# Cross-attention on one core: values of two quads in one run, rows of x by halves in one room, output-projection steps dealt anew

## The chip, the cores and the metric

The kernel runs on one core of one Trainium2 chip. The metric is the device time of one launch in microseconds (us), the median of several runs. All data are 32-bit floats.

The engines go by the names of the profile: PE is TensorE (matrix products), PEld its weight loads, DVE is VectorE, ACT is ScalarE, POOL is GpSimd, and SP is SyncE, whose queue issues nearly all DMA transfers. Each engine runs its own instructions in the order in which the program gives them, and waits by semaphores for what other engines hand it.

## The reference

Eight batches of 256 rows with 1024 features; 32 heads of 32 features each. `ctx` serves as keys and as values.

```python
xn = (x - mean(x)) * rsqrt(var(x) + 1e-5) * gamma + beta
Q  = split_heads(xn @ Wq.T)                     # 8 x 32 heads x 256 x 32
K = V = split_heads(ctx)
scores = einsum('bhsd,bhtd->bhst', Q, K) / sqrt(32), masked over t
attn   = einsum('bhst,bhtd->bhsd', softmax(scores), V)
out    = x + merge_heads(attn) @ Wout.T         # 8 x 256 x 1024
```

## The kernel before

**Quads and slots.** Four heads (128 features) are a *quad*; a batch has eight, all batches 64. The main loop (`for n in range(N)`, N = 64) does one *slot* per quad. The code writes i for the slot's place in its batch of output work: b, i = divmod(n - 8, 8). The order of instructions on every engine is written out by hand (the pool's scheduler is off). In slot n TensorE does, in this order:

1. `scores(n + 1)` (L493): scores of the next quad, 8 matmuls into the four banks of `ps_s`;
2. `project_steps(n, 0)`;
3. `values(n - 2)` (L643): softmax times V of the quad two slots back, 64 matmul records in the trace, into the two banks of `ps_v`;
4. `project_steps(n, 1)`;
5. in slots i = 2 to 7 and 0 `query_product` (L216, tile `pq`): one of the seven products that make Q for a later batch;
6. behind the softmax of quad n + 1 in the program, `project_steps(n, 2)`.

**Projections.** Both projections are done by a scheme with seven products of half-size blocks (A11, A12, S2, S3, A22, S1, S4, in this order for the output), with sums of blocks formed on GpSimd (`sum_at`, `sum_x`). The output projection of a batch is 28 *steps* (seven products of four chunks; a step is one call of `product`, L216, tile `po`), dealt over the nine slots that follow the batch's attention. `STEPS[i]` says how many steps stand at places 0, 1 and 2 of slot i:

```python
STEPS = ((0, 0, 0), (0, 7, 0), (0, 1, 2), (0, 2, 2), (0, 2, 1), (0, 1, 2), (0, 0, 3), (0, 1, 2),
         (0, 2, 0))
```

All products of the output share one bank (`ps_o`) and, for the first, the bank of `ps_q`. Between products the sum is evacuated: `keep_p1` (ScalarE, L735, slot i = 1), `take` and `store` (VectorE, L765 and L769, slots 2, 3, 4, 6, 7, 8; store(1,0) in i = 6, store(1,1) in i = 7). The batch before the last (b = 6) has its own deal, `ENDS`, its own evacuation by `copy_po` (ScalarE, L745, slots 59 to 63), and the last batch's steps (`po_last`, `po_end`) stand in slots 59 to 62 and after the loop.

**Softmax.** `softmax(n + 1)` runs in slot n. VectorE: eight reductions that add the mask and find the row's extreme (L531), reciprocals (L542), four block transposes `blocks` into pT (L556), the evacuations above, the query copies `copy_product` (L475, L470), the mask (`mask_bias`, L483, at the end of slots i = 6). ScalarE: exponentials (L535), `copy_at` (L656), which takes the finished values of a quad out of `ps_v` right behind the first exponentials, and `aside` (L562), a copy of half of pT into `pc`. GpSimd: the normalization (L550). The tail of a softmax (last transpose, last copy aside, and on SP's queue the moves between pT and pc, L621 and L625, with the loads of k, L135, and v, L143) stands at its end; for quads after 56 it is held back into the next softmax.

**Rows of x.** Every batch's x passes through: load (L129), statistics (`ln_stats`, L234 to L239, on VectorE, 1.6 us for a half of 128 rows), normalization (`ln_norm`, L255, ScalarE), block transposes into `xe` (`blocks_x`, L323, VectorE), and sixteen moves into xnT on SP's queue (`move_x`, L339, in slots first - 6 to first - 4). `first` = 8(b - 1) + 2 is the slot of the batch's first query product. The tables `loads`, `stats`, `norms`, `trans`, `moves` and `at_end` give the slot of each, per half s = 0, 1. x and xe take turns in two rooms of a pool `xp` of 8 KB per partition each.

Of the kernel before, what the change touches and what calls it, by code (L numbers as in the profile page):

```python
# [46 lines left out]
F32 = mybir.dt.float32  # L47
# [12 lines left out]
def xattn_kernel(  # L60
# [25 lines left out]
    N = B * NQ  # L86

    const = ctx.enter_context(tc.tile_pool(name="const", bufs=1))
    xp = ctx.enter_context(tc.tile_pool(name="xp", bufs=2))
    rp = ctx.enter_context(tc.tile_pool(name="rp", bufs=4))  # L90
    lnp = ctx.enter_context(tc.tile_pool(name="lnp", bufs=2))
    kp = ctx.enter_context(tc.tile_pool(name="kp", bufs=2))
# [1 line left out]
    atp = ctx.enter_context(tc.tile_pool(name="atp", bufs=3))  # L94
    ep = ctx.enter_context(tc.tile_pool(name="ep", bufs=4))
    ptp = ctx.enter_context(tc.tile_pool(name="ptp", bufs=3))
    asp = ctx.enter_context(tc.tile_pool(name="asp", bufs=3))
    up = ctx.enter_context(tc.tile_pool(name="up", bufs=1))
    sm = ctx.enter_context(tc.tile_pool(name="sm", bufs=8))
    dram = ctx.enter_context(tc.tile_pool(name="dram", bufs=1, space=bass.MemoryType.DRAM))  # L100
# [18 lines left out]
        nc.tensor.transpose(busy, ident, ident)  # L119


    xs, ks, vs, rs = {}, {}, {}, {}

    def load_x(b, s, h=None, queue=nc.sync):

        if b not in xs:
            xs[b] = xp.tile([P, NS, D], F32, tag="x", name=f"x_{b}")
        cols = ds(0, D) if h is None else ts(h, 512)
        queue.dma_start(xs[b][:, s, cols], x[b, ts(s, P), cols])  # L129

    def load_k(n):

# [91 lines left out]
    def ln_stats(b, s, parts=range(3), later=None):  # L224


        if s == 0 and 0 in parts:
            mvs[b] = sm.tile([P, NS, 2], F32, tag="mv", name=f"mv_{b}", bufs=2)
            rstds[b] = sm.tile([P, NS], F32, tag="rstd", name=f"rstd_{b}", bufs=2)
        if 0 in parts:  # L230
            sts[b, s] = sm.tile([P, 2, 6], F32, tag="st", name=f"st_{b}_{s}", bufs=2)
        for h in range(2):
            if h in parts:
                nc.vector.bn_stats(sts[b, s][:, h, :], xs[b][:, s, ts(h, 512)])  # L234
        if 2 not in parts:
            return
        nc.vector.bn_aggr(mvs[b][:, s, :], sts[b, s].rearrange("p h k -> p (h k)"))
        ve = sm.tile([P, 1], F32, tag="ve", name=f"ve_{b}_{s}", bufs=2)
        nc.vector.tensor_scalar(ve, mvs[b][:, s, 1:2], LN_EPS, None, ALU.add)  # L239

        def pow_():
            nc.gpsimd.tensor_tensor(rstds[b][:, s : s + 1], ve, mhalf[:, :1], ALU.pow)

        if later is None:
            pow_()
        else:
            later.append(pow_)

    def ln_norm(b, s, engine):
        if engine is nc.scalar:  # L250
            shift = sm.tile([P, 1], F32, tag="shift", name=f"shift_{b}_{s}", bufs=2)
            nc.gpsimd.tensor_scalar(
                shift, mvs[b][:, s, 0:1], rstds[b][:, s : s + 1], -1.0, ALU.mult, ALU.mult
            )
            engine.activation(  # L255
                xs[b][:, s, :], xs[b][:, s, :], AF.Identity,
                bias=shift, scale=rstds[b][:, s : s + 1],
            )
            return
        engine.tensor_scalar(  # L260
            xs[b][:, s, :], xs[b][:, s, :], mvs[b][:, s, 0:1], rstds[b][:, s : s + 1],
            ALU.subtract, ALU.mult,
        )

# [4 lines left out]
    def transpose_x0(s, diag=None):  # L269

        pool, tag, k = (ps_v, "pv", NC // 2) if diag is None else (ps_s, "sc", 2)
        for g in range(NC // k):
            pt = pool.tile([P, k, P], F32, tag=tag, name=f"px0_{s}_{g}")
            for i in range(k):
                px0[s, k * g + i] = pt[:, i, :]
                chunk = xs[0][:, s, ts(k * g + i, P)]
                if diag is None:
                    nc.tensor.transpose(pt[:, i, :], chunk, ident)
                else:
                    nc.tensor.matmul(pt[:, i, :], chunk, diag, start=True, stop=True)  # L280
# [24 lines left out]
    def transpose_x1(p):  # L305

        if p == 0:
            tile_ = lnp.tile([P, NC * (S + 1)], F32, tag="xnT", name="xnT_1")
            px1["to"] = tile_[:, : NC * S].rearrange("p (c t) -> p c t", c=NC)
            xnTs[1] = lambda c: px1["to"][:, c, :]  # L310
        pt = px1[p] = ps_v.tile([P, 2, S], F32, tag="pv", name=f"px1_{p}")
        for i in range(2):
            for s in range(NS):
                nc.tensor.transpose(pt[:, i, ts(s, P)], xs[1][:, s, ts(2 * p + i, P)], ident)  # L314

    def copy_x1(p):
        nc.scalar.copy(px1["to"][:, ts(p, 2), :], px1.pop(p))
# [1 line left out]
    def blocks_x(b, s):  # L319

        if s == 0:
            xes[b] = xp.tile([P, NA, NC, NS, K], F32, tag="x", name=f"xe_{b}")
        nc.vector.transpose(  # L323
            xes[b][:, :, :, s, :],
            xs[b][:, s, :].rearrange("p (c q k) -> p q c k", c=NC, q=NA),
        )

    def move_x(b, part):
# [178 lines left out]
    def softmax_parts(n, copies=(), ahead=(), between=(), hooks={}, fill=()):  # L507
# [9 lines left out]
                fill.pop(0)()  # L517

        pss = scs[n]
        pT = pTs[n] = ptp.tile([P, 2, NI, NH, NS, K], F32, tag="pT", name=f"pT_{n}")  # L520
        pc = asp.tile([P, NI, NH, NS, K], F32, tag="pc", name=f"pc_{n}")
        es, mns, dens = {}, {}, {}

        def exps(j, part=range(NS)):
# [107 lines left out]
            tail()  # L632
        yield

    def values(n):
        pvs[n] = [
            ps_v.tile([P, 2, NS, K], F32, tag="pv", name=f"pv_{n}_{r}") for r in range(2)
        ]
        pT = pTs.pop(n)
        for i in range(NI):  # L640
            for j in range(NH):
                for r in range(2):
                    nc.tensor.matmul(  # L643
                        pvs[n][r][j * HD : (j + 1) * HD],
                        vs[n - n % 2][ts(r, 2 * K), i, ds(n % 2 * P + j * HD, HD)],
                        pT[ts(r, 2 * K), :, i, j, :, :],
                        start=(i == 0), stop=(i == NI - 1),
                    )

    def copy_at(n):  # L650
        b, c = divmod(n, NQ)
# [3 lines left out]
        for r, pv in enumerate(pvs.pop(n)):  # L655
# [19 lines left out]
    P1_ASIDE = (0, 1, 2, 3, 4, 5)  # L675
    STEPS = ((0, 0, 0), (0, 7, 0), (0, 1, 2), (0, 2, 2), (0, 2, 1), (0, 1, 2), (0, 0, 3), (0, 1, 2),
             (0, 2, 0))
    ENDS = ((0, 0, 2), (0, 0, 5), (0, 0, 5)) + ((0, 0, 4),) * 4 + ((0, 0, 0),)
    ENDS_TO = {2: (0, 0), 3: (0, 1), 4: (1, 1), 5: (1, 0), 6: (1, 1), 7: (0, 1)}

    def steps_of(b):
        if b == B - 2:
            return ENDS
        return STEPS

    assert all(sum(map(sum, steps_of(b))) == len(PRODUCTS) * NK for b in range(B - 1))

# [200 lines left out]


    ln_stats(0, 0)  # L890
    x0 = xs[0][:, 0, :]
    mean = mvs[0][:, 0, 0:1]
    nc.vector.tensor_scalar(x0, x0, mean, None, ALU.subtract)
    diag = ring[:, 0, 1, :]
# [53 lines left out]
    for n in range(N):  # L948
# [19 lines left out]
        if n in (2, 4):  # L968
            between.append(partial(load_wo, B21, n // 2 - 1))
        if n == N - 4:  # L970
            again = xp.tile([P, NS, D], F32, tag="x", name="x_again")
            for s in range(NS):
                between.append(partial(nc.sync.dma_start, again[:, s, :], x[B - 1, ts(s, P), :]))

# [8 lines left out]
                place = 0 if i in (3, 4, 6) or i < 3 and what is not add_p1 else "soon" if i == 2 else 1  # L983
                hooks.setdefault(place, []).append(partial(what, one, *args))
        if n >= 2:
            values(n - 2)
        project_steps(n, 1)
        copies = [partial(copy_q, q) for q in new_q]
        if n in halves and n % 2 == 0:
# [26 lines left out]
                make_q(q)  # L1016
                copy_q(q)
        else:
            copy_at(n - 2)
# [160 lines left out]
```

## Time and profile before

| | |
|---|---|
| runs | 563.6, 563.45, 562.49 us; median 563.45 |
| profiled execution | 562.29 us, its span 560.5 us |
| granted TensorE clock | 1.00 |
| busy: PE, DVE, ACT, POOL | 555.1, 466.3, 423.7, 392.9 us |
| DMA moved | 119.30 MB, mean 213 GB/s |

A row of a timeline gives the start in us from the start of the span, the duration, engine, source line, operation, output<-inputs by the program's names, shapes, and how many instructions (x16) were taken together; in square brackets stands the idle time ahead and what ended it. The 32-bit matmuls show as several records each: sixteen records are one `scores`, four are one step of the output projection. Matmuls are pipelined, so a row's duration runs over into the next row's; what a run occupies is read from start to start.

### The profile page before, as it was taken

How to read it: one execution, taken by the hardware profiler on the slowest of the kernel's cores; microseconds unless marked ns; L12 is line 12 of the kernel's file. 1: busy time of each engine (PE TensorE's matmuls, PEld its weight loads, DVE VectorE, ACT ScalarE, POOL GpSimd, SP SyncE). 2: the span in 40 equal slices, each digit the busy share in tenths (PEclk: the TensorE clock that was granted, in tenths of full speed). 3: DMA queues.
4: the chain of work that ended last, by engine and by line, in shares of the span. 5: the costliest groups of instructions: out<-in, count | busy, mean ns of one | idle time of the engine just before them, and what ended most of it. 6: DMA issues, size and time to landing. Idle time of an engine off the chain costs nothing.

```text
span 560.5 us, 24339 instructions
## 1 busy us (share of the span) xinstructions
PE 555.1 (99%) x9334; PEld 357.0 (64%) x9334; DVE 466.3 (83%) x1716; ACT 423.7 (76%) x1464; POOL 392.9 (70%) x635
## 2 busy tenths in 40 slices
PE   8999999999999999999999999999999999999997
PEld 7666665767656767567765676566766766744443
DVE  5979889999998888988898888988888878879823
ACT  3699999998769867797777877778776876869920
POOL 1688887999797666867568666777648657448780
PEclk9999999999999999999999999999999999999999
DMA  8967657957678767877778767788667874536752
GB/s 305 397 188 209 184 150 235 319 179 223 207 253 246 246 183 223 259 204 232 217 232 233 207 186 233 221 233 239 176 166 249 244 228 130 149 91 182 209 169 76
DMA packets 47236, 119.30 MB, mean 213 GB/s; under 512 B 8976, under 2 KB 9744, under 8 KB 47120
## 3 DMA queue, kind: packets, MB, share of 16 engines
q1 hardware_dynamic: 46832, 117.48, 69.5%
q8 instruction: 74, 1.21, 1.0%
q14 instruction: 42, 0.34, 0.2%
q10 hardware_dynamic: 288, 0.27, 0.1%
HBM read 66.33 MB, written 11.53 MB: 139 GB/s over the span
## 4 chain that ended last, share of the span: by engine, by line
PE 98%; DVE 1%; DMA 1%; ACT 0%; POOL 0%; issue 0%; POOLq 0%
PE po_S L216 20%; PE pq_A L216 19%; PE pv L643 12%; PE sc L493 12%; PE po_A L216 11%; PE pq L216 10%; PE pq_S L216 7%; PE po_end L216 3%; PE po_last L216 1%; DMA x<-in_x_dram 1%; PE po_end_s L216 0%; PE px L280 0%; PE px L314 0%; ACT e L535 0%; DVE st L234 0%; DVE xnT L289 0%
## 5 line engine op out<-in xcount | busy, mean ns | idle before, releaser
L550 POOL TENSOR_SCALAR e<-e,rden 128x256 f32<-128x256 f32 x466 | 215.5, 479 | 124.2 <-DVE rden L542 121.7
L535 ACT ACTIVATE e<-e,mn 128x256 f32<-128x256 f32 x512 | 254.0, 501 | 43.6 <-DVE mn L531 43.1
L556 DVE STREAM_TRANSPOSE pT<-e 128x512 f32<-128x512 f32 x256 | 178.9, 703 | 36.6 <-POOL e L550 27.5
L531 DVE CUSTOM_DVE_ANT_0 e<-sc,mb 128x256 f32<-128x256 f32 x512 | 185.3, 416 | 23.8 <-PE sc L493 23.3
L562 ACT COPY pc<-pT 128x512 f32<-128x512 f32 x128 | 78.9, 616 | 52.2 <-DVE pT L556 34.5
L535 ACT ACTIVATION_READ_ACCUMULATOR e<-e,mn 128x1 f32 x512 | 98.2, 192 | 0.0
L493 PEld LDWEIGHTS sc<-k,qa 32*128 32x128 f32 x1024 | 46.1, 184 | 45.6 <-issue 22.4
L643 PE MATMUL pv<-pT,v 64*32 64x128 f32 x4096 | 74.2, 274 | 0.0
L493 PE MATMUL sc<-k,qa 32*128 32x256 f32 x1024 | 73.6, 400 | 0.2 <-ACT qa L301 0.2
L216 PE MATMUL po_S<-wo,at 128*64 128x512 f32 x304 | 73.5, 598 | 0.0
L643 PEld LDWEIGHTS pv<-pT,v 64*32 64x32 f32 x4096 | 57.1, 105 | 22.7 <-issue 9.6
L216 PE MATMUL po_A<-wo,at 128*64 128x512 f32 x256 | 58.6, 598 | 0.0
L216 PE MATMUL pq<-xnT,wq 128*64 128x256 f32 (+3 forms) x544 | 58.4, 369 | 0.0
L216 PEld LDWEIGHTS pq_A<-xnT,wq 128*64 128x64 f32 x832 | 46.3, 137 | 7.4 <-issue 6.3
L216 PE MATMUL po_S<-wo,s 128*64 128x512 f32 x208 | 49.5, 598 | 0.0
L216 PEld LDWEIGHTS pq<-xnT,wq 128*64 128x64 f32 x544 | 36.8, 136 | 18.9 <-issue 1.8
L216 PE MATMUL pq_A<-xnT,wq 128*64 128x128 f32 x832 | 47.6, 273 | 0.0
L542 DVE RECIPROCAL rden<-den 128x2 f32<-128x2 f32 x256 | 38.3, 150 | 5.8 <-ACT e L535 4.9
L531 DVE DVE_READ_ACCUMULATOR2_ANT mn<- 128x1 f32 x512 | 42.6, 83 | 0.0
L216 PEld LDWEIGHTS po_A<-wo,at 128*64 128x64 f32 x256 | 16.9, 136 | 30.0 <-issue 29.1
L216 PEld LDWEIGHTS po_S<-wo,at 128*64 128x64 f32 x304 | 19.3, 136 | 22.6 <-issue 22.6
L656 ACT COPY at<-pv 128x128 f32<-128x128 f32 x128 | 26.2, 254 | 8.7 <-PE pv L643 8.7
(99 smaller groups left out, 645.4 us busy)
## 6 DMA issues: line engine op xcount, KB each, us to landing
v<-in_kv_dram SPq DMA_DIRECT2D x32, 512.0 KB, 4.8
pT<-pT SPq DMA_DIRECT2D x128, 128.0 KB, 3.3
pT<-pc SPq DMA_DIRECT2D x128, 128.0 KB, 4.1
ring<-kept_T SPq DMA_DIRECT2D x20, 512.0 KB, 5.3
k<-in_kv_dram SPq DMA_DIRECT2D x32, 256.0 KB, 4.0
x<-in_x_dram SPq DMA_DIRECT2D x15, 512.0 KB, 6.6
r<-in_x_dram SPq DMA_DIRECT2D x28, 256.0 KB, 5.1
out_dram<-r SPq DMA_DIRECT2D x28, 256.0 KB, 2.6
```

The lines of the kernel that those rows point to most:

```text
L216: nc.tensor.matmul(out[ts(w, P // 2)], stationary[:, ts(w, P // 2)], moving, **flags)
L493: nc.tensor.matmul(scs[n][j][:, s, :], qa[r, n % NQ, ts(s, P)], ks[n - n % 2][r, n % 2, :], start=True, stop=True,)
L531: nc.vector.tensor_tensor_reduce(out=e[:, s, :], in0=pss[j][:, s, :], in1=mbs[n // NQ], scale=1.0, scalar=NO_SCORE, op0=ALU.add, op1=ALU.m ...
L535: nc.scalar.activation(e[:, s, :], e[:, s, :], AF.Exp, bias=mn[:, s : s + 1], scale=-1.0, accum_out=den[:, s : s + 1],)
L542: nc.vector.reciprocal(rden, dens[j])
L550: engine.tensor_scalar(es[j][:, s, :], es[j][:, s, :], rden[:, s : s + 1], 1.0, ALU.mult, ALU.mult,)
L556: nc.vector.transpose(pT[:, :, :, j, :, :].rearrange("p a i s k -> p (a i) s k"), es[j].rearrange("p s (b t) -> p b s t", t=K),)
L562: nc.scalar.copy(pc[:, :, ts(j, 2)], pT[:, 1, :, ts(j, 2)])
L643: nc.tensor.matmul(pvs[n][r][j * HD : (j + 1) * HD], vs[n - n % 2][ts(r, 2 * K), i, ds(n % 2 * P + j * HD, HD)], pT[ts(r, 2 * K), :, i, j, ...
L656: nc.scalar.copy(ats[b, k][:, c, :, ts(r, 2), :], pv.rearrange("p a s k -> p s a k"))
```

## The change

1. **Paired values.** Quads 20 to 61 (`PAIRED`) are done two in one run, in odd slots n from 23 on: `due(n)` gives (n - 3, n - 2) there and nothing in the even slots 22 to 62. The two quads share the two banks, each in its half; `copy_at` takes both out in the odd slot. All other quads are done as before.
2. **Steps dealt anew.** Batches from 2 on use `STEPS_PAIRED`. In batch 6 the block sum S2 is formed in two equal parts, at the ends of slots i = 0 and i = 1, instead of three quarters and one.
3. **Rooms.** One constant tile `rooms` of five halves (4 KB per partition each) takes the place of the pool `xp`. Batch 1 has rooms 0 and 1, batches 0, 2 and 3 have rooms 2 and 3; from batch 4 on (`HALVED`) both halves use room 2, one after the other; xe, and x loaded again for the last batch, lie in rooms 0 and 1. pT of quads 23, 27, ..., 63 (`SPARE`) lies in rooms 3 and 4, and pc of quads 2, 5, ..., 17 in room 4. The pool of pc has two buffers instead of three.
4. **Times of the rows of x.** From batch 4 on: loads at the ends of slots first - 14 and first - 10 (before: among the transfers of the softmax in first - 13 and first - 12, for batch 4 first - 14 and first - 13), statistics in first - 12 and first - 8 (before - 11 and - 9), normalization in first - 11 and first - 7 (before - 8 and - 7), transposes in first - 10 and first - 6 (before - 7 and - 6). The moves stay.

```diff
-    xp = ctx.enter_context(tc.tile_pool(name="xp", bufs=2))
-    asp = ctx.enter_context(tc.tile_pool(name="asp", bufs=3))
+    asp = ctx.enter_context(tc.tile_pool(name="asp", bufs=2))
...
+    rooms = const.tile([P, 5, D], F32, tag="x", name="rooms")
+    HALVED = 4
+
+    def x_rows(b, s):
+        return rooms[:, (0 if b == 1 else 2) + (s if b < HALVED else 0), :]
...
-        pT = pTs[n] = ptp.tile([P, 2, NI, NH, NS, K], F32, tag="pT", name=f"pT_{n}")
-        pc = asp.tile([P, NI, NH, NS, K], F32, tag="pc", name=f"pc_{n}")
+        if n not in SPARE:
+            pTs[n] = ptp.tile([P, 2, NI, NH, NS, K], F32, tag="pT", name=f"pT_{n}")
+        else:
+            pTs[n] = rooms[:, 3:].rearrange("p a (i j s k) -> p a i j s k", i=NI, j=NH, s=NS)
...
-    def values(n):
-        pvs[n] = [
-            ps_v.tile([P, 2, NS, K], F32, tag="pv", name=f"pv_{n}_{r}") for r in range(2)
+    PAIRED = range(20, N - 2)
+    SPARE = range(23, N, 4)
+
+    def due(n):
+        if n - 2 not in PAIRED:
+            return (n - 2,)
+        return (n - 3, n - 2) if n % 2 else ()
+
+    def values(*quads):
+        if not quads:
+            return
+        banks = [
+            ps_v.tile([P, len(quads), 2, NS, K], F32, tag="pv", name=f"pv_{quads[0]}_{r}")
+            for r in range(2)
         ]
+        for u, n in enumerate(quads):
+            pvs[n] = [bank[:, u] for bank in banks]
...                                              # the loops over i, j, r as before, for each quad
+    STEPS_PAIRED = ((0, 0, 0), (0, 6, 0), (0, 2, 2), (0, 2, 1), (0, 3, 1), (0, 0, 3), (0, 0, 4),
+                    (0, 0, 1), (0, 3, 0))
...
-        return STEPS
+        return STEPS if b < PAIRED[0] // NQ else STEPS_PAIRED
...
-                loads=(first - 12, first - 11) if b == SPLIT + 1 else (first - 13, first - 12),
-                stats=(first - 10, first - 8) if b == SPLIT + 1 else (first - 11, first - 9),
-                norms=(first - 8, first - 7), trans=(first - 7, first - 6),
+                loads=(first - 12, first - 11) if b < HALVED else (),
+                stats=(first - 10, first - 8) if b < HALVED else (first - 12, first - 8),
+                norms=(first - 8 if b < HALVED else first - 11, first - 7),
+                trans=(first - 7 if b < HALVED else first - 10, first - 6),
...
-        if b == SPLIT + 2:
-            loads[first - 13], loads[first - 12] = [(b, 1)], []
-            at_end[first - 14].append((b, 0))
+        if b >= HALVED:
+            for i in range(NS):
+                at_end[first - 14 + 4 * i].append((b, i))
...
-            values(n - 2)
+            values(*due(n))
...
-            sum_at(b, "S2", *((slice(NK - 1, NK),) if b == B - 2 else ()))
+            sum_at(b, "S2", *((slice(NK // 2, NK),) if b == B - 2 else ()))
...
-                sum_at(b, "S2", slice(0, NK - 1))
+                sum_at(b, "S2", slice(0, NK // 2))
```

More of the change, by code (lines that the diff above doesn't have):

```diff
@@ L119, in xattn_kernel @@
         nc.tensor.transpose(busy, ident, ident)
-    xs, ks, vs, rs = {}, {}, {}, {}
+    ks, vs, rs = {}, {}, {}
+    rooms = const.tile([P, 5, D], F32, tag="x", name="rooms")
+    HALVED = 4
+    def x_rows(b, s):
+        return rooms[:, (0 if b == 1 else 2) + (s if b < HALVED else 0), :]
     def load_x(b, s, h=None, queue=nc.sync):
-        if b not in xs:
-            xs[b] = xp.tile([P, NS, D], F32, tag="x", name=f"x_{b}")
         cols = ds(0, D) if h is None else ts(h, 512)
-        queue.dma_start(xs[b][:, s, cols], x[b, ts(s, P), cols])
+        queue.dma_start(x_rows(b, s)[:, cols], x[b, ts(s, P), cols])
     def load_k(n):
@@ L233, in ln_stats @@
             if h in parts:
-                nc.vector.bn_stats(sts[b, s][:, h, :], xs[b][:, s, ts(h, 512)])
+                nc.vector.bn_stats(sts[b, s][:, h, :], x_rows(b, s)[:, ts(h, 512)])
         if 2 not in parts:
@@ L255, in ln_norm @@
             engine.activation(
-                xs[b][:, s, :], xs[b][:, s, :], AF.Identity,
+                x_rows(b, s), x_rows(b, s), AF.Identity,
                 bias=shift, scale=rstds[b][:, s : s + 1],
@@ L260, in ln_norm @@
         engine.tensor_scalar(
-            xs[b][:, s, :], xs[b][:, s, :], mvs[b][:, s, 0:1], rstds[b][:, s : s + 1],
+            x_rows(b, s), x_rows(b, s), mvs[b][:, s, 0:1], rstds[b][:, s : s + 1],
             ALU.subtract, ALU.mult,
@@ L275, in transpose_x0 @@
                 px0[s, k * g + i] = pt[:, i, :]
-                chunk = xs[0][:, s, ts(k * g + i, P)]
+                chunk = x_rows(0, s)[:, ts(k * g + i, P)]
                 if diag is None:
@@ L313, in transpose_x1 @@
             for s in range(NS):
-                nc.tensor.transpose(pt[:, i, ts(s, P)], xs[1][:, s, ts(2 * p + i, P)], ident)
+                nc.tensor.transpose(pt[:, i, ts(s, P)], x_rows(1, s)[:, ts(2 * p + i, P)], ident)
     def copy_x1(p):
@@ L321, in blocks_x @@
         if s == 0:
-            xes[b] = xp.tile([P, NA, NC, NS, K], F32, tag="x", name=f"xe_{b}")
+            xes[b] = rooms[:, :2].rearrange("p r (a c s k) -> p (r a) c s k", a=2, c=NC, s=NS)
         nc.vector.transpose(
             xes[b][:, :, :, s, :],
-            xs[b][:, s, :].rearrange("p (c q k) -> p q c k", c=NC, q=NA),
+            x_rows(b, s).rearrange("p (c q k) -> p q c k", c=NC, q=NA),
         )
@@ L519, in softmax_parts @@
         pss = scs[n]
-        pT = pTs[n] = ptp.tile([P, 2, NI, NH, NS, K], F32, tag="pT", name=f"pT_{n}")
-        pc = asp.tile([P, NI, NH, NS, K], F32, tag="pc", name=f"pc_{n}")
+        if n not in SPARE:
+            pTs[n] = ptp.tile([P, 2, NI, NH, NS, K], F32, tag="pT", name=f"pT_{n}")
+        else:
+            pTs[n] = rooms[:, 3:].rearrange("p a (i j s k) -> p a i j s k", i=NI, j=NH, s=NS)
+        pT = pTs[n]
+        if n < PAIRED[0] and n % 3 == 2:
+            pc = rooms[:, 4].rearrange("p (i j s k) -> p i j s k", i=NI, j=NH, s=NS)
+        else:
+            pc = asp.tile([P, NI, NH, NS, K], F32, tag="pc", name=f"pc_{n}")
         es, mns, dens = {}, {}, {}
@@ L633, in softmax_parts @@
         yield
-    def values(n):
-        pvs[n] = [
-            ps_v.tile([P, 2, NS, K], F32, tag="pv", name=f"pv_{n}_{r}") for r in range(2)
-        ]
[L639 to L648, printed above, removed]
+    PAIRED = range(20, N - 2)
[10 more added lines that the diff above has]
+            for r in range(2)
+        ]
+        for u, n in enumerate(quads):
+            pvs[n] = [bank[:, u] for bank in banks]
+            pT = pTs.pop(n)
+            for i in range(NI):
+                for j in range(NH):
+                    for r in range(2):
+                        nc.tensor.matmul(
+                            pvs[n][r][j * HD : (j + 1) * HD],
+                            vs[n - n % 2][ts(r, 2 * K), i, ds(n % 2 * P + j * HD, HD)],
+                            pT[ts(r, 2 * K), :, i, j, :, :],
+                            start=(i == 0), stop=(i == NI - 1),
+                        )
     def copy_at(n):
@@ L890, in xattn_kernel @@
     ln_stats(0, 0)
-    x0 = xs[0][:, 0, :]
+    x0 = x_rows(0, 0)
     mean = mvs[0][:, 0, 0:1]
@@ L970, in xattn_kernel @@
         if n == N - 4:
-            again = xp.tile([P, NS, D], F32, tag="x", name="x_again")
+            again = rooms[:, :2]
             for s in range(NS):
@@ L1018, in xattn_kernel @@
         else:
-            copy_at(n - 2)
+            for done in due(n):
+                copy_at(done)
             tails.pop()()
```

## The prediction

> **What bounds the kernel now.** Read first: the page's head, its busy shares and the chain that ended last, then the waits of the tensor engine.
>
> ```profile
> span 560.5 us, 24339 instructions
> PE 555.1 (99%) x9334; PEld 357.0 (64%) x9334; DVE 466.3 (83%) x1716; ACT 423.7 (76%) x1464; POOL 392.9 (70%) x635
> PE 98%; DVE 1%; DMA 1%; ACT 0%; POOL 0%; issue 0%; POOLq 0%
> ```
> ```profile
> PE px L280 <- DVE ring L895: 1.0, 1, 1.0
> PE sc L493 <- ACT qa L301: 0.2, 1, 0.2
> ```
>
> TensorE is busy 99% of the span, the chain is TensorE for 98%, and the waits found are in the prologue. From there to the end no matmul waits: time is the sum of TensorE's runs, and every other engine has cover. So two questions decide: does the change shorten TensorE's runs, and does a matmul now come due before its data?
>
> **Part 1: values of two quads in one run.** The timeline of TensorE; the two lines from slot 0 show a slot without values.
>
> ```profile
> 22.96 1.15 PE L493 MATMUL sc<-k,qa 32*128 32x256 f32 x16
> 24.04 3.70 PE L216 MATMUL pq<-xnT,wq 128*64 128x257 f32 x32
> ...
> 239.53 1.15 PE L493 MATMUL sc<-k,qa 32*128 32x256 f32 x16
> 240.61 1.16 PE L643 MATMUL pv<-pT,v 64*32 64x128 f32 x64
> 240.74 1.02 PE L643 MATMUL pv<-pT,v 64*32 64x128 f32 x56
> 241.29 0.48 PE L643 MATMUL pv<-pT,v 64*32 64x128 f32 x16
> 241.70 1.94 PE L216 MATMUL po_S<-wo,s 128*64 128x512 f32 x8
> ```
>
> The run of 64 occupies 241.70 − 240.61 = 1.09 us from start to start. Inside it, with 56 matmuls left at 240.74 and 16 at 241.29, 40 take 0.55, so 64 take 0.88. The rest, 0.21, goes with entering and leaving the run. Scores take 1.08 whether values follow (239.53 to 240.61) or a projection (22.96 to 24.04), so leaving a run out costs nothing else. 42 quads (20 to 61) become 21 pairs; each pair saves 0.21: 21 × 0.21 = **−4.4 us**. A paired run is 1.09 + 0.88 = 1.97.
>
> [...]
>
> **Part 2: the slots shift.** Slots are counted from the start of scores. Even slots from 22 on lose 1.09, odd ones gain 0.88, and the re-dealt projection steps (0.86 to 0.89 each: the twelve records from 204.25 to 206.93 below are three steps in 2.68) even this out: by sums of runs, slots i = 0 to 7 of batches 2 to 5 become 7.3, 8.3, 8.2, 9.3, 8.2, 9.3, 8.2, 7.5. Whoever feeds TensorE and isn't moved with it may come late. I went through each matmul that needs an evacuated bank; the ones that come out late:
>
> (a) *Slot 15.* The statistics of batch 4 move from slot 15's end to slot 14's, on VectorE ahead of the reductions.
>
> ```profile
> 139.94 1.15 PE L493 MATMUL sc<-k,qa 32*128 32x256 f32 x16
> 143.01 3.66 PE L216 MATMUL pq_A<-xnT,wq 128*64 128x128 f32 x64
> 146.50 1.89 PE L216 MATMUL po_S<-wo,at 128*64 128x512 f32 x8
> ...
> 141.41 0.42 DVE L531 CUSTOM_DVE_ANT_0 e<-sc,mb 128x256 f32<-128x256 f32 x1
> 145.34 0.65 DVE L769 TENSOR_TENSOR r<-po_S,r 128x512 f32<-128x512 f32 x1
> 148.66 1.25 DVE L234 BATCH_NORM_STATS2 st<-x 128x6 f32<-128x512 f32 x2
> 150.26 0.41 DVE L531 CUSTOM_DVE_ANT_0 e<-sc,mb 128x256 f32<-128x256 f32 x1
> ```
>
> The statistics hold VectorE 150.26 − 148.66 = 1.60. The store that empties the bank (L769) ends at 145.99 and would end at 147.59; the S4 step that refills that bank is due at 146.50: **1.1**.
>
> (b) *Slots 31 and 39*, where the statistics of batches 6 and 7 now precede the reductions.
>
> ```profile
> 341.02 1.15 PE L493 MATMUL sc<-k,qa 32*128 32x256 f32 x16
> 341.25 0.51 DVE L483 TENSOR_SCALAR mb<-mk 128x256 f32<-128x256 uint8 x1
> 342.18 0.42 DVE L531 CUSTOM_DVE_ANT_0 e<-sc,mb 128x256 f32<-128x256 f32 x1 [0.42 <-PE sc L493]
> 346.11 0.65 DVE L769 TENSOR_TENSOR r<-po_S,r 128x512 f32<-128x512 f32 x1
> ```
>
> VectorE is free 0.23 into slot 39 today; slot 38 gets 0.23 shorter, so I take 0.35. Then 1.60 of statistics, 0.51 of mask: reductions start at 2.46 instead of 1.16. From first reduction to end of store is 346.76 − 342.18 = 4.58, so the bank is empty at 7.04. S4 is due at 1.08 + 1.97 + 0.05 + 3.49 (products: 146.50 − 143.01) = 6.59: 0.45, say **0.5 each, 1.0**.
>
> (c) and (d) *Slot 22 and its like*, where values vanish and everything behind them is due 1.09 sooner.
>
> ```profile
> 198.55 1.15 PE L493 MATMUL sc<-k,qa 32*128 32x256 f32 x16
> 204.25 2.75 PE L216 MATMUL po_S<-wo,s 128*64 128x512 f32 x12
> 206.93 1.15 PE L493 MATMUL sc<-k,qa 32*128 32x256 f32 x16
> ...
> 202.53 0.69 DVE L769 TENSOR_TENSOR r<-po_S,r 128x512 f32<-128x512 f32 x1
> 205.96 0.65 DVE L475 TENSOR_TENSOR qa<-pq_A,qa 128x512 f32<-128x512 f32 x1
> ```
>
> The query copy (L475) ends 206.61 − 198.55 = 8.06 into the slot, and only the second half of the next scores reads it. Slot 22 shrinks from 8.38 to 7.29; that half begins 0.54 later, less the weights that load ahead: **0.5** (0.2 to 0.8). In slots 30, 38, 46 and 54, S1's first step is due at 204.25 − 1.09 = 203.16, the store ends at 203.22 and TensorE takes some hundredths to resume: **0.1 each, 0.4**.
>
> (e) and (f) *The last batch*, whose slots have little work.
>
> ```profile
> 505.94 1.15 PE L493 MATMUL sc<-k,qa 32*128 32x256 f32 x16
> 507.43 0.41 DVE L531 CUSTOM_DVE_ANT_0 e<-sc,mb 128x256 f32<-128x256 f32 x1
> 512.54 1.15 PE L493 MATMUL sc<-k,qa 32*128 32x256 f32 x16
> 513.49 0.58 ACT L745 COPY ends<-po_A 128x512 f32<-128x512 f32 x1
> 525.75 1.15 PE L493 MATMUL sc<-k,qa 32*128 32x256 f32 x16
> 533.55 0.43 ACT L656 COPY at<-pv 128x128 f32<-128x128 f32 x2
> ```
>
> Slots of 6.60 (512.54 − 505.94) become 7.48 and 5.52. VectorE's work of slot 58 doesn't shrink, so in slot 59 the reductions start near 2.57, not 1.49, and copy_po (L745), 1.53 into slot 60 at its end, comes 1.1 later against a slot start 0.88 later: 1.8. The A22 step that reuses the bank is due at 1.13 once values are gone: 0.7, with the resume **0.75**. At the end, the copy of attention ends 8.23 behind 525.75; the first step that reads it is due at 5.52 + 1.97 + 0.05 = 7.54: **0.75**.
>
> Each of these ten waits (1, 2, 1, 4, 1 and 1) restarts a run: 0.05 each, **0.5**; that 0.05, here and in (b) and (f), is my estimate for starting a run, a quarter of the 0.21 of part 1 (bounds 0 and 0.1).
>
> **Part 3: rooms for x.** Same bytes and as many transfers, so nothing by itself. From batch 4 on a half of x can load only once the half before it is transposed out of the room (L323), so both loads now stand at ends of slots, i = 4 and 0, the first behind four moves of xnT on SP's queue; its statistics follow two slots later.
>
> ```profile
> DMA to landing us min/median/max: 5.2/6.6/7.7
> ...
> 398.74 2.43 SPq L339 DMA_DIRECT2D xnT<-xe  x4
> 401.27 2.33 SPq L621 DMA_DIRECT2D pT<-pT  x2
> ...
> 399.64 1.15 PE L493 MATMUL sc<-k,qa 32*128 32x256 f32 x16
> ...
> L323 DVE STREAM_TRANSPOSE xe<-x 128x1024 f32<-128x1024 f32 x12 | 14.5, 1206 | 0.0
> ```
>
> The queue lags by more than a slot: the four moves that slot 44 issues at its end leave from 398.74 on, around the start of slot 46 (399.64), and are through at 401.17. A load behind them starts 1.6 into a slot i = 6 and lands 6.6 later, at 8.2 (at most 9.3). The statistics at that slot's end start 0.35 behind its 8.15, at 8.5. I price the wait at 0, because 0.3 remains at the median; without that cover VectorE stands still and (b) grows (rival 2). Transposes (1.2 each) and normalizations move whole to other slots, which is no more work. VectorE is busy 7.1 of 8.4 us in slot 39 below, and the eight reductions, from 342.18 at 0.42 each, are through by 345.5, 3.9 before the next scores need their banks at 349.40: reductions 1.6 late stay hidden from the scores. Spare rooms for pT and two copies aside (asp) instead of three: what they wait for are SP's transfers, gone from the queue 401.27 + 2.33 − 399.64 = 4.0 into a slot, and a room is wanted again two slots later or more: nothing. What moving the statistics may save where they stood I also take as 0, since TensorE waited in none of those slots.
>
> ```profile
> 341.02:349.40 8.38, 8.38 (x159) 5.88 (x157) 7.13 (x27) 6.64 (x24) 4.26 (x9) 1.00 0.76 225
> ```
>
> (Columns: length; busy PE, PEld, DVE, ACT, POOL; clock; DMA share; GB/s.)
>
> **The sum.** −4.4 + 1.1 + 1.0 + 0.5 + 0.4 + 0.75 + 0.75 + 0.5 = **+0.6 us**. The profiled execution took 562.29 (span 560.5 and 1.8 around it): 562.9. It lies 1.16 below the median of the runs, 563.45: on the median **564.1**.
>
> **Rivals.**
> 1. *The waits mostly don't come; faster.* Each of (a) to (f) rests on VectorE or ScalarE keeping its order and lag; where they catch up, only (a) and part of (c) and (f) stay, 1.5 to 2. Then 563.45 − 4.4 + 1.8 = 560.9. For it: TensorE's gain is measured inside one run, and the gaps in (b), (d) are tenths. Against it: by the row of slot 39 VectorE has 1.2 us free in a slot, so it doesn't catch up 1.6 at once.
> 2. *Late rows of x; slower.* If rows land at 9.3 or with the queue some tenths later still, and not at 8.2, the statistics and the eight reductions behind them start 0.8 to 1.2 later in slots 31 and 39, and S4 waits for the store by as much: up to +2.4, 566.5. It decides from a landing 0.3 later than the median. For it: half of all x landings lie between the median and 1.1 above it. Against it: the queue is read in one slot of another batch, and may be ahead there.
> 3. *The pairing doesn't do what it says:* the second quad costs 1.09 in the run (a new 128-column accumulation in the same bank); only the waits stay: 563.45 + 5.0 = 568.4, 567.3 at a quarter of the gain.
>
> **How the numbers follow.** Forecast (gain given back by waits; its own range 562.6 to 565.4, from waits of 3.6 to 6.4): 0.42. Rival 1: 0.25. Rival 2, with other delays of VectorE: 0.30. Rival 3: 0.03. A difference of 0.2% is 1.1 us, about what this kernel's measurement can tell from no change. Faster takes rival 1, slower rivals 2 and 3: 0.25, 0.42, 0.33. The range runs from rival 1's 560.9 to just above rival 2's 566.5.
>
> **What would show it.** In the changed kernel's trace: paired runs of 128 matmuls of 1.97 (2.18 would be rival 3); waits of TensorE on VectorE's L769 store in slots 15, 31, 39, on qa before slot 23's scores, on ScalarE's copy in slot 60 and on at at the end, 5 us in all with few others. Rival 1 shows less than 2 us; rival 2 shows VectorE waiting for a DMA ahead of the statistics. I am wrong if scores wait for their banks in many slots, for which slot 39 leaves 3.9 us.

## The result and the profile after

The changed kernel takes 585.2 us (580.19 to 588.18, 4 runs) against 563.44 before: ratio 1.038 (1.035 to 1.041). It is 22 us slower; forecast was no change, 564.1, with a range that ends just above 566.5. Executions over 1.5% longer than the fastest of the same kernel are left out of the medians and ratios (two of the four of experiment 2, one of experiment 12). The profiled execution took 584.33, its span 582.5, 22.0 more than before.

The page of the changed kernel: span, busy shares, chain, the instruction queue among the DMA queues.

```profile
span 582.5 us, 24362 instructions
PE 561.9 (96%) x9334; PEld 363.8 (62%) x9334; DVE 466.6 (80%) x1716; ACT 424.1 (73%) x1464; POOL 394.3 (68%) x635
q8 instruction: 73, 1.20, 0.9%
PE 36%; issue 1%; DVE 1%; ACT 0%; POOL 0%; DVEq 0%
```

As many matmuls as before, but TensorE now idles 20.6 us instead of 5.4, and is busy 6.8 us longer although pairs should have shortened it. The chain's shares no longer add up to the span (it breaks off), so it says nothing here; the waits of TensorE do (total us, times, longest):

```profile
PE pq_A L217 <- issue: 6.3, 3, 3.5
PE po_S L217 <- POOL wo L183: 2.3, 1, 2.3
PE po_S L217 <- DVE r L794: 2.2, 4, 1.1
PE po_A L217 <- issue: 1.6, 1, 1.6
...
PE pq_S L217 <- DMA ring<-kept_T: 0.9, 1, 0.9
PE pv L666 <- issue: 0.8, 1, 0.8
...
PE po_S L217 <- issue: 0.7, 1, 0.7
PE po_end L217 <- ACT at L679: 0.4, 1, 0.4
```

Of these, 9.4 us are "issue": TensorE waits for nothing that the profile shows, no data and no bank. I had no such term. The longest, in the timeline of TensorE in slot 37:

```profile
330.58 1.15 PE L494 MATMUL sc<-k,qa 32*128 32x256 f32 x16
331.65 1.16 PE L666 MATMUL pv<-pT,v 64*32 64x128 f32 x64
332.55 1.21 PE L666 MATMUL pv<-rooms,v 64*32 64x128 f32 x64
333.69 3.50 PE L217 MATMUL pq_A<-sx,wq 128*64 128x128 f32 x60
340.67 0.70 PE L217 MATMUL pq_A<-sx,wq 128*64 128x128 f32 x4 [3.49 <-issue]
341.15 4.16 PE L217 MATMUL po_S<-wo,at 128*64 128x512 f32 x12
```

A product stops after 60 of its 64 records, in the middle of a run whose operands have all been in use. So it isn't data; what is left to look at is the instructions. The instruction queue q8 moved 73 packets, 1.20 MB, 16 KB each. TensorE has 18,877 instructions in the trace (matmuls, weight loads, semaphores), 259 for each packet, 63 bytes each by these sums; by the stops' numbers below, I take a packet for a block of 256, which makes 64 bytes. Here are the DMA queues from 326 us to 338 (the stop begins at 337.2), then of 338 to 339.4 (kind, packets, MB, share):

```profile
DMA packets 1156, 3.24 MB, mean 270 GB/s; under 512 B 205, under 2 KB 205, under 8 KB 1154
q1 hardware_dynamic: 1154, 3.22, 91.9%
q14 instruction: 2, 0.02, 0.4%
```
```profile
DMA packets 72, 0.14 MB, mean 97 GB/s; under 512 B 17, under 2 KB 17, under 8 KB 71
q1 hardware_dynamic: 71, 0.12, 31.6%
q8 instruction: 1, 0.02, 5.5%
```

From 326 to 338 no block of q8 came, while data filled 92% of the DMA engines; the next came once TensorE had stopped, and TensorE resumed 1.4 us behind it. Counted along TensorE's instructions, the six "issue" waits stand at numbers 8642, 11202, 13505, 15297, 16577 and 17602: each 193 or 194 beyond a multiple of 256. TensorE runs out of instructions at the border of a block. A pair is 128 matmul records and 128 weight loads: one whole block, used up in 2 us. Leaving the waits out, the fastest blocks from 150 us on take 4.8, 4.8 and 5.4 us before, and 2.1, 2.2 and 2.3 after; ten take under 3.6. Speed is not all of it, though. The block that ends in the longest stop takes 4.7 us without that stop, no less than the fastest before; there the next packet began only 5.6 us behind the border of the block. A stop came here where the next packet landed too late for its block, and the six stops have both sides: in slot 45 a block of 2.3 us whose next packet began 2.3 behind the border, in slot 37 this one of 4.7 with 5.6.

Before, 74 such packets came and no wait of TensorE is put down to "issue"; after, 73 came and six waits are.

The two longest stops cost once more. The window behind the first (columns as before):

```profile
341.15:345.25 4.10, 4.10 (x16) 1.10 (x13) 1.31 (x2) 0.62 (x1) 0.03 (x1) 0.65 0.50 116
```

Its granted clock averages 0.65: 3.41 us at half clock from 340.59 on (and again from 408.86), 1.7 us lost each time; the twelve records at 341.15 take 4.1 instead of 2.7.

**The account of the 22.0**, TensorE's work piece by piece against the same piece before: instruction waits 9.4, half clock 3.4, restarts and slow runs around them about 2; slot 15 4.1 (it lasts 12.47 instead of 8.38); late stores in slots 23, 31, 39 1.6; S1's first step, due just ahead of its store, five times 0.2; a late transfer into `ring` in slot 34 1.1; the last steps, which wait for the copy of attention, 0.5; pairs −3.2. That is 19.9; the other 2 I can't place.

### The profile page after: what moved, and what is told of

Its sections match the earlier page's. It is cut to its first block, busy times and chain, and to the rows that moved or that the text cites. A ratio compares the mean times of both kernels' runs of the same rounds, so it can differ in the third digit from the quotient of the medians.

```text
span 582.5 us, 24362 instructions
## 1 busy us (share of the span) xinstructions
PE 561.9 (96%) x9334; PEld 363.8 (62%) x9334; DVE 466.6 (80%) x1716; ACT 424.1 (73%) x1464; POOL 394.3 (68%) x635
## 5 line engine op out<-in xcount | busy, mean ns | idle before, releaser
L564 DVE STREAM_TRANSPOSE pT<-e 128x512 f32<-128x512 f32 x212 | 147.9, 703 | 30.9 <-POOL e L558 25.0
L570 ACT COPY pc<-pT 128x512 f32<-128x512 f32 x94 | 57.9, 617 | 48.5 <-DVE pT L564 28.4
L217 PE MATMUL po_S<-wo,at 128*64 128x512 f32 x304 | 74.8, 609 | 2.3 <-DVE r L794 2.2
L217 PE MATMUL po_A<-wo,at 128*64 128x512 f32 x256 | 59.9, 599 | 1.6 <-issue 1.6
L666 PE MATMUL pv<-pT,v 64*32 64x128 f32 x3392 | 59.2, 273 | 0.0
L666 PEld LDWEIGHTS pv<-pT,v 64*32 64x32 f32 x3392 | 47.9, 105 | 14.9 <-issue 8.4
L217 PEld LDWEIGHTS po_S<-wo,at 128*64 128x64 f32 x304 | 20.7, 139 | 29.3 <-issue 25.0
L564 DVE STREAM_TRANSPOSE rooms<-e 128x512 f32<-128x512 f32 x44 | 31.1, 706 | 7.0 <-POOL e L558 7.0
```

The source lines that it names most:

```text
L217: nc.tensor.matmul(out[ts(w, P // 2)], stationary[:, ts(w, P // 2)], moving, **flags)
L564: nc.vector.transpose(pT[:, :, :, j, :, :].rearrange("p a i s k -> p (a i) s k"), es[j].rearrange("p s (b t) -> p b s t", t=K),)
L570: nc.scalar.copy(pc[:, :, ts(j, 2)], pT[:, 1, :, ts(j, 2)])
L666: nc.tensor.matmul(pvs[n][r][j * HD : (j + 1) * HD], vs[n - n % 2][ts(r, 2 * K), i, ds(n % 2 * P + j * HD, HD)], pT[ts(r, 2 * K), :, i, j, ...
```

## The experiments

Theory 1: paired runs use up a block of instructions faster than the next one arrives. Rival: the moved rows of x crowd the DMA engines, and the fetch of instructions with them. Beside them stands the question what slot 15 waits for. Each median and ratio is taken against the kernel before on the same chip (563.3 to 563.6).

**1. No pairs.**

```diff
-        if n - 2 not in PAIRED:
-            return (n - 2,)
-        return (n - 3, n - 2) if n % 2 else ()
+        return (n - 2,)
...
-        return STEPS if b < PAIRED[0] // NQ else STEPS_PAIRED
+        return STEPS
```

> The changed kernel with values one quad at a time in every slot and the old deal of steps; rooms and times of x stay changed. Theory 1 (TensorE runs out of instructions: a run of 128 value matmuls with their 128 weight loads uses up a whole 16 KB block of instructions in 2 us, faster than the next block comes): the waits put down to 'issue' fall from 9.4 us to under 0.5, and no half clock follows; what stays are the waits of slot 15 (3.9 us, GpSimd held by rstd and the late store) and about 1 us in slots 31 and 39: 563.4 + 5 = 568. Rival (the moved loads of x crowd the DMA engines and hold up the fetch of instructions by themselves): waits of the kind 'issue' stay at 5 us or more, 575 or more.

574.1 us, ratio 1.020 (1.016 to 1.023). No "issue" wait is left, as theory 1 says. (The old deal of steps came back together with the single quads; experiment 4 parts the two.) But the time is 6 above what I expected of it. VectorE and TensorE around slot 31:

```profile
278.77 0.69 DVE L564 STREAM_TRANSPOSE rooms<-e 128x512 f32<-128x512 f32 x1
282.12 1.29 DVE L235 BATCH_NORM_STATS2 st<-rooms 128x6 f32<-128x512 f32 x2 [2.66 <-DMA rooms<-in_x_dram]
...
289.04 3.56 PE L217 MATMUL po_S<-wo,at 128*64 128x512 f32 x8 [3.16 <-DVE r L792]
```

This is the prediction's second rival, larger than priced: statistics wait 2.66 for rows of x, the store is late, S4 waits 3.16, and half clock follows (8 records in 3.56); slot 15's wait is followed by half clock here too. In the full change this load left 4.0 us into slot 30 instead of 5.5 and landed just in time: at 280.11, with the statistics starting at 280.13. That TensorE's stop in slot 29 gave it this time is argued, not tested.

**2. The borders shifted.** Behind the prologue's transposes:

```diff
+    for i in range(32):
+        nc.tensor.matmul(busy[ts(i % 4, 32), :], ident[:64, ts(i % 4, 32)], ident[:64, :], start=True, stop=True)
```

> The changed kernel with 32 small matmuls (128 TensorE instructions, half a block) added behind the 26 transposes of the prologue. Theory 1: the blocks' borders fall elsewhere against the paired runs, so the 'issue' waits move: today they stand in slots 29, 37, 45, 51 and 59; with the shift most of their time is in others (by the borders read from the trace: 25, 27, 31, 43, 47, 53, 61); the sum may be anything from 5 to 15 us, the time 575 to 595. Rival (the slot's own transfers decide): the waits stay in slots 29, 37, 45, 51, 59 and the time is 586 to 587.

580.9, 1.031 (1.027 to 1.036). Seven "issue" waits, 8.5 us, in slots 25, 29, 37, 43, 47, 51 and 53. Four of these, with 4.8 us, had none before (all four among the seven that I had named); the others are where waits stood already. They come at instruction numbers 7617, 8898, 11202, 12994, 14273, 15554 and 16065, all again 193 or 194 beyond a multiple of 256, though 128 instructions stand ahead of them. The border goes along with the count, not with the place in the work.

**3. Batch 4's rows as before.**

```diff
-    HALVED = 4
+    HALVED = 5
...
-                stats=(first - 10, first - 8) if b < HALVED else (first - 12, first - 8),
+                stats=(first - 10, first - 8) if b == SPLIT + 1 else (first - 11, first - 9) if b < HALVED else (first - 12, first - 8),
...
+        if b == SPLIT + 2:
+            loads[first - 13] = [(b, 1)]
+            at_end[first - 14].append((b, 0))
```

> The changed kernel with batch 4's rows of x treated as before (two halves in two rooms, its loads, statistics, normalization and transposes in their old slots). If slot 15's waits come from the statistics moved to slot 14 (GpSimd's rstd, which waits for them, stands ahead of its sums of weights), the 2.3 us on wo and the 1.1 us on the store go, and about 4 us of the time: 581. Rival (they come from the copies aside that lie in another room, or from the loads): they stay, 585. The block borders don't move, so the other waits stay where they are.

583.64, 1.034 (1.028 to 1.040): 1.6 less, not 4. In the profiled execution the instruction waits were 11.2 instead of 9.4, and half clock took 1.7 more; and with executions from 577 to 585 the difference of the medians is within the scatter. What the experiment shows is in the rows: slot 15's two waits are gone. GpSimd in the changed kernel, then TensorE, VectorE and TensorE again:

```profile
136.90 1.91 POOL L558 TENSOR_SCALAR e<-e,rden 128x256 f32<-128x256 f32 x4
142.76 0.55 POOL L243 TENSOR_TENSOR rstd<-ve,mhalf 128x1 f32<-128x1 f32 x1 [3.95 <-DVE ve L240]
143.28 1.27 POOL L183 TENSOR_TENSOR wo<-wo 128x512 f32<-128x512 f32 x1
...
144.61 1.08 PE L217 MATMUL po_S<-wo,s 128*64 128x512 f32 x4 [2.29 <-POOL wo L183]
...
149.21 0.71 DVE L564 STREAM_TRANSPOSE pT<-e 128x512 f32<-128x512 f32 x1 [3.07 <-POOL e L558]
149.85 0.65 DVE L794 TENSOR_TENSOR r<-po_S,r 128x512 f32<-128x512 f32 x1
...
150.56 1.94 PE L217 MATMUL po_S<-wo,at 128*64 128x512 f32 x8 [1.14 <-DVE r L794]
```

The statistics' last piece, rstd (L243), runs on GpSimd. It waited 3.95 for VectorE, and behind it stood the sum of output weights that S1 needs in slot 15, three sums of query weights and the normalization of the next quad. VectorE waited 3.07 for that normalization, so the store behind it (L794) came late too.

**4. Runs of 128 in the kernel before**, nothing of x touched:

```diff
             values(n - 2)
+            if n % 2 and 22 < n < N:
+                values(n - 2, True)
...                                              # with True, values keeps its operands and its banks
```

> The kernel before, with values computed twice in a row in slots 23, 25, ... 63 (same operands, same banks: the second time overwrites the first with the same); nothing of x or of the steps is changed. The added work is 21 runs of about 0.88 to 0.95 us: 18.5 to 20. Theory 1: runs of 128 value matmuls alone bring 'issue' waits of 4 us or more, in some of these slots: 586 or more. Rival (only the moved transfers of x bring them): no such waits, 582 to 583.5.

591.2, 1.051 (1.046 to 1.055), in the range of theory 1. Four "issue" waits, 5.7 us, all at such borders. One of them:

```profile
298.44 2.03 PE L643 MATMUL pv<-pT,v 64*32 64x128 f32 x128
300.40 0.64 PE L216 MATMUL po_A<-wo,at 128*64 128x512 f32 x1
303.74 1.50 PE L216 MATMUL po_A<-wo,at 128*64 128x512 f32 x6 [2.70 <-issue]
```

Runs of 128 bring the stops by themselves, without the moved transfers and without the new deal of steps; the rival as it stood is out.

**5. The load of x ahead of the moves of xnT**, without pairs (from 1):

```diff
-        for args in moves[n]:
-            move_x(*args)
         for args in at_end[n]:
             load_x(*args)
+        for args in moves[n]:
+            move_x(*args)
```

> The kernel without pairs (574.1), with the load of a half of x put ahead of the moves of xnT at a slot's end instead of behind them. There x was issued 5.5 us into slot 30 and landed at 282.1; VectorE waited 2.7 for it, the store in slot 31 came late, TensorE waited 3.2 for it and then ran 3.4 us at half clock. If late rows of x cause that, the load starts some 3.6 earlier, VectorE doesn't wait, and 4.9 us go: 569. Rival (the statistics' own 1.6 us and the mask ahead of the reductions do it, the load is incidental): TensorE's wait in slot 31 stays above 2, 573 to 574.

570.26, 1.011 (1.008 to 1.014): 3.8 less. VectorE's row now has no wait, and slot 31's wait is 0.35:

```profile
278.70 1.24 DVE L235 BATCH_NORM_STATS2 st<-rooms 128x6 f32<-128x512 f32 x2
```

**6. No rows of x for batches 4 to 7.** Their entries in `at_end`, `stats` and `norms` are left out.

> The changed kernel with loads, statistics and normalization of x left out for batches 4 to 7 (transposes and moves stay, on old rows). 4 MB of transfers go; TensorE's instructions and their blocks are the same. The waits on VectorE's store and on GpSimd's weights go in either case (5 us). If only the rate at which a paired run uses up a block counts, the 'issue' waits stay near 9 us in the same slots: 578 to 581. If the fetch also waits behind the rows of x in the DMA engines (in slot 37 its packet started 5.6 us after its block's border), the waits in slots 37 and 45 shrink from 3.5 and 2.6 to under 1.7 each, the sum falls to about 5, no half clock follows, and the time is 571 to 574.

578.56, 1.028 (1.023 to 1.034). The same point of slot 37 as above:

```profile
333.72 3.50 PE L217 MATMUL pq_A<-sx,wq 128*64 128x128 f32 x60
337.96 0.44 PE L217 MATMUL pq_A<-sx,wq 128*64 128x128 f32 x4 [0.75 <-issue]
```

Slot 37 went from 3.49 to 0.75, slot 45 from 2.65 to 1.37, and no half clock followed. In slot 37 the packet now began 2.9 us behind the border instead of 5.6. But there are ten waits now, 10.2 us in all. So the rows of x lengthen single fetches; that there are stops at all, they don't decide. Over half clock this says little: a wait of 2.1 in slot 33 went without it here, and one of 1.9 brought it in experiment 3. How the sum divides between short blocks and late packets isn't settled by this.

**7. Borders set away from the pairs** (184 instructions ahead of 3), and **8.** the same with 5's order and the store of slots i = 6 earlier:

```diff
+    for i in range(46):
+        nc.tensor.matmul(busy[ts(i % 4, 32), :], ident[:64, ts(i % 4, 32)], ident[:64, :], start=True, stop=True)
...
-                place = 0 if i in (3, 4, 6) or i < 3 and what is not add_p1 else "soon" if i == 2 else 1
+                place = 0 if i in (3, 4) or i == 6 and n < 22 or i < 3 and what is not add_p1 else "soon" if i in (2, 6) else 1
```

> The kernel with batch 4's rows as before (583.6), with 46 small matmuls (184 TensorE instructions) added in the prologue, so that by the borders read from the traces few paired runs begin just behind a border. Theory (blocks of 256 instructions, fetched in about 4 us from border to resumption): 'issue' waits fall from 11.2 us to 2 to 4, none long enough for half clock, every one at an instruction whose number in TensorE's stream is 193 or 194 beyond a multiple of 256: 566 to 570. Rival (the borders play no part, transfers alone do): 9 us or more stay, 580 to 585.

> As the one before, and the load of x ahead of the moves of xnT, and the store of slot i = 6 (from slot 22 on) after the second instead of the fourth pair of reductions, so that S1's first step need not wait for it (0.2 us in five slots). Pairs then keep 3.1 us of gain against about 0.8 of waits on stores, 0.5 at the end and 2 to 3 of instruction waits: 562 to 567; about 1 to 2 below the one before. If the waits moved elsewhere: no difference from it.

581.43 (1.030, 1.026 to 1.034) and 577.18 (1.026, 1.021 to 1.032): both missed. In 7, no block takes under 2.66 us, and 7.4 us of "issue" remain in four waits instead of 2 to 4; the longest, 3.29, stands in a block that takes 4.9 without it: as long as the fastest blocks of the kernel before, which never waited. In 8, the "issue" waits come to 7.9 us. The about 4 us from border to resumption were my assumption; in the six stops of the changed kernel it is 2.8 to 8.2, over the stops in all traces 2.8 to 9.2. Placing the borders doesn't cure it. In 7, values and a product also waited for transfers (1.5 and 2.4); in 8 these waits are 0.2.

**9. What is left without pairs**: 5 and 3 together.

> No pairs, old deal of steps, loads of x ahead of the moves (570.3 so far), and batch 4's rows as before; what is left of the change is rooms, halves in one room from batch 5 on, and two copies aside. If slot 15's two waits (2.3 on GpSimd's sums of weights, 1.1 to 1.5 on the store) come from batch 4's statistics alone, they go: 566.4. What stays are waits of 0.4 to 0.6 on the store in slots 23, 31, 39 and a few of some tenths. If the rooms or the copies aside cost something by themselves, waits of values on their transfers show: 568 or more.

566.15, 1.006 (1.003 to 1.008), 4.1 under 5, as expected of slot 15. Of the waits on the store 0.5 is left in all; one of 1.2 of values on a copy aside is new. What is left of the change costs 2.5 us and gains nothing by itself.

**10. to 12.** With 3's and 5's edits: pairs in one run (10); apart in their slot, with the steps of place 1 between them or the query product where there are none (11, first edit); and besides, the second quad's copy at the end of the softmax (12, second edit):

```diff
         for u, n in enumerate(quads):
+            if u and between:
+                between()
...
+        if n:
+            for done in list(pvs):
+                copy_at(done)
```

> The changed kernel with batch 4's rows as before and loads of x ahead of the moves; pairs in one run. Base for the next: 578 to 583, 'issue' waits 8 to 11 us, all at instruction numbers 193 or 194 beyond a multiple of 256.

> As the one before, but in slots 23 to 55 the two quads of a pair stand apart in the same slot, with the slot's steps of place 1 between them, or its query product where it has no such steps; slots 59 to 63 have nothing to put between and stay. Each of the 17 pairs loses its saving (0.15): +2.6. If it is the run that empties a block in 2 us, 'issue' waits fall to 3 us or less (slot 59's 1.6 stays) and no half clock follows: 569 to 573. If the slot's sum of instructions counts, wherever they stand, 7 us or more stay and the time is 580 or above.

> The pairs apart in their slot again, and now the copy of the second quad stands at the end of the softmax on ScalarE; ahead of the second exponentials it held ScalarE until that quad's values were done (64 us of waits in all) and with it the whole softmax, so that the run before this one said little. In that run the fastest block of 256 instructions of slots 23 to 55, waits left out, lasted 3.8 us, against 2.1 with adjacent pairs and 4.9 in the kernel before. If the time of a block decides, 'issue' waits are 2 to 5 us (the pairs of slots 59 to 63 are still adjacent), ScalarE's waits for values vanish, and the time is 568 to 574. If the number of value instructions in a slot decides, wherever they stand, 8 us or more stay: 577 or more.

581.55 (1.029, 1.024 to 1.034), 620.22 (1.101, 1.095 to 1.107) and 613.2 (1.090, 1.085 to 1.095). "Issue" waits: 15.1, 7.9 and 3.0 us. The first two are above what I expected (8 to 11, and 3 or less). The third is in the range that I gave for blocks stretched out (none under 3.8 in slots 23 to 55), but 11's blocks are as long there and it stops all the same: its 2.3 us in slot 43 end a block that takes 6.3 without them, because the packet began 6.1 behind the border. So a long block alone doesn't protect. The times of 11 and 12 are far off. ScalarE says why, here in the last of them:

```profile
ACT at L684 <- PE pv L671: 64.6, 19, 5.9
```
```profile
224.63 1.16 PE L671 MATMUL pv<-pT,v 64*32 64x128 f32 x64
231.02 1.16 PE L671 MATMUL pv<-rooms,v 64*32 64x128 f32 x64
232.22 0.43 ACT L684 COPY at<-pv 128x128 f32<-128x128 f32 x2 [3.67 <-PE pv L671]
```

In the kernel before, this copy waits 8.7 us in all. The two quads share a bank, and the copy of the first quad (values at 224.63) still waited until the second (231.02) was done: 64.6 us against 64.1 in the one before. My edit moved the wrong copy, so these two kernels say something of instruction waits and nothing of what pairs apart would cost. Pairs with x as before were not tried: the pairs' additional pT lies in the rooms that x gave up. No version ran faster than the kernel before.

## Why the prediction was wrong

**What bounds it.** "Time is the sum of TensorE's runs" was right for the kernel before; what failed is the sentence "two questions decide". I asked of every run whether its data would be there and never whether its instructions would, so the sum has no term for TensorE's supply of instructions: it was put at nothing without a reason. The page had the numbers: 18,668 matmuls and weight loads and 74 instruction packets of 16 KB, a block per 7.6 us on average. A pair asks for one in 2 us. The missing term measured 9.4 us of waits, some 15 with half clock and restarts; pairs and their deal of steps cost 11.1 (585.2 against 574.1), or 15.4 with the other faults mended (581.55 against 566.15).

**Part 1.** −4.4 came out as −3.2 (21 times 0.15). An undisturbed pair; 13 of the 21 take 2.03 or 2.04:

```profile
314.17 2.10 PE L666 MATMUL pv<-pT,v 64*32 64x128 f32 x128
316.20 1.94 PE L217 MATMUL po_S<-wo,s 128*64 128x512 f32 x8
```

2.03 from start to start, not 1.97: 0.15 saved, not 0.21. I had read 0.88 for 64 matmuls off the middle of a run. Rival 3 is out: it wanted 2.18. The quarter of the gain at which it also prices itself (567.3) is a share that no run shows; the pairs kept 0.15 of the 0.21.

**Part 2.** The slots' lengths came out as summed where nothing waited: 7.3, 8.4, 8.2, 9.3, 8.2 and 7.6 in slots 40 to 44 and 47, for 7.3, 8.3, 8.2, 9.3, 8.2 and 7.5.

**(a)** 1.1 for slot 15; measured 4.1 with restarts. I followed VectorE only. The step "VectorE ahead of the reductions" left out rstd on GpSimd and what is queued behind it.

**(b)** 0.5 each: 0.5 and 0.4 with restarts in the full change. That was luck: I had the load start 1.6 us into its slot, from one row of another batch; in slot 30 it started 4.0 in and landed 0.02 ahead of the statistics. Without pairs it started 5.5 in, and slot 31 cost 4.9 (experiments 1 and 5). The rival was named with the right mechanism and priced at half.

**(c)** 0.5 on the query copy: TensorE didn't wait for it in slot 23; instead the store there made it wait 0.50, which I hadn't on the list. **(d)** 0.1 each: 0.2 each. **(e)** 0.75 in slot 60: nothing in the full change, where slot 59's instruction wait gave ScalarE the time, and 0.8 in experiments 2, 7 and 8, where that wait was absent. **(f)** 0.75: 0.36 of wait, 0.5 with the restart.

**Part 3** at 0: experiment 9 leaves 2.5 (1.5 to 4.7 by the interval) for rooms, halves from batch 5 on and times, once order and batch 4 are mended.

Without the instruction term the account comes to +5.1, and 2 that I can't place, not +0.6: about 568.5 to 570.5, still above the range, which ends just above 566.5. That leaves out the late rows of experiment 1, which the change with its stops did not show. Of the rivals, 2 came out once the stops were gone (experiment 1), 1 and 3 did not; none held an engine that stops without a reason in the data, so the range had no room for it.

## What to carry to other kernels

Where TensorE is at 99%, ask of a denser run not only whether operands and banks are ready but how many instructions per us it takes, block by block, against the fastest block that runs today, and how long the DMA queues hold back the next packet; here runs of 128 short matmuls with 128 weight loads, in 2.03 us, left TensorE without instructions (9.4 us of waits). When an instruction moves, follow each piece of it on every queue: here a tiny power on GpSimd, put ahead of sums of weights, cost more than the 1.6 us of VectorE that it came from. And when a stop is removed, look at what it covered: late rows of x (experiment 1) and a late copy in slot 60 (experiments 2, 7 and 8) appeared only then.

## What the runs showed of the hardware

- Of 70 "issue" waits of over 0.12 us from 150 us on, in eleven kernels, 68 stand at TensorE instructions 193 or 194 beyond a multiple of 256. At these TensorE resumes 1.2 to 1.7 us behind the end of the 16 KB packet, which itself takes 0.9 to 1.7; from border to packet it takes from 0.2 us (slot 55 of the changed kernel) to 5.6 (its slot 37, data on 92% of the DMA engines) and 6.8 (experiment 12).
- Half clock came in stretches of 3.41 us (or twice that). The shortest wait that one followed was 1.9 us (experiment 3), but longer ones went without: of experiment 8's waits of 2.43, 2.20 and 2.68 only the 2.20 brought it, and the changed kernel's 2.29 in slot 15 did not. The two stretches of the changed kernel begin 68.27 us apart. What decides it, no run here shows.
- With two quads in one bank, the copy of the first waited for the last matmul of the second, not for its own half (64.6 us in experiment 12). Whether the chip asks for that or only the semaphores of this program, no run here shows.
